# Row sums from ones beside the values, and the key masks prepared inside self attention, in a two-layer decoder kernel

## The chip, the cores and the metric

The kernel runs on one core of one Trainium2 chip, as a single launch. The metric is the device time of one execution in microseconds (us); the time given for a kernel is the median of its runs. The profile comes from one execution that the hardware profiler recorded. Its engines are PE (the matrix engine; PEld is its weight load), DVE (VectorE), ACT (ScalarE), POOL (GpSimd) and SP (SyncE, which here only issues transfers).

## The reference, cut to what matters

A decoder of two layers works on 4 batches of 256 tokens by 256 features, with 1601 memory tokens for each batch. Layer 0 is self attention, attention over the memory and a quantised feed-forward; layer 1 is a recurrence, cross attention and experts. The change lies in layer 0's first two parts:

```python
def _L0_attn_ref(x, ...):                 # 16 heads of 16
    q = (_layernorm(x, qn_g, qn_b) @ Wq + bq)...
    kv = (_layernorm(x, kvn_g, kvn_b) @ Wkv + bkv)...
    k, v = (kv[0], kv[1])
    q = _rotary(q * scale, x); k = _rotary(k * scale, x)
    qn = _layernorm(q, ln_g, ln_b)
    kn = _layernorm(k, ln_g, ln_b)
    scores = jnp.einsum('bhqd,bhkd->bhqk', qn, kn) / jnp.sqrt(hd)
    scores = jnp.where(causal, scores, jnp.finfo(scores.dtype).min)
    w = jax.nn.softmax(scores, axis=-1)
    a = jnp.einsum('bhqk,bhkd->bhqd', w, v)
    return a.transpose(0, 2, 1, 3).reshape(B, C, Dm) @ Wo + bo

def _L0_xattn_ref(hidden_states, memory_tokens, memory_mask):
    scores = jnp.einsum('bsd,bmd->bsm', hidden_states, memory_tokens) * scale
    scores = jnp.where(memory_mask[:, None, :], scores, neg_inf)
    attn = jax.nn.softmax(scores, axis=-1)
    readout = jnp.einsum('bsm,bmd->bsd', attn, memory_tokens)
    valid_b = jnp.any(memory_mask, axis=-1)
    return jnp.where(valid_b[:, None, None], readout, jnp.zeros_like(readout))
```

## The kernel before, in words

Everything of a batch stays on the chip: `xs[b]` holds its 256 tokens as two blocks of 128 partitions. For each batch a Python generator `before(b)` (L934) emits self attention (L336), memory attention (L524), feed-forward (L633) and recurrence (L694), one stage between two `yield`s. A loop of ticks takes one stage of each running generator per tick; the batches start at ticks 0, 3, 9 and 15 (`START`). Three further streams are woven in: `shared_weights` (L303) from tick `TERN` = 20 on, the position tables and the first head's keys of layer 1's cross attention (`angles`, L959, and `before_head`, L1128) from tick `SIDE` = 24 on, and then the cross attention's heads and the experts, which are about four fifths of the time.

The order of the work on each engine is not the order in which it is written. The tile framework's scheduler puts instructions into the engines' queues from the order of emission, the data and the free buffers; each queue then runs strictly in that order. `behind` (L1344) ties everything that one stage of a stream emits behind the instruction that each engine was given last, so that the scheduler can't pull it forward. `shared_weights` and the position streams go through it.

Self attention of a batch, in stages:

- Statistics, normalisation, and transposes to features (L342 to L359).
- The query and key product `pq` and its bias add `qk` (L367, L371), the value product `pv` and its add `v` (L377, L381). Rotary and the norm of every head follow on VectorE and POOL (L391 to L415).
- Transposes to `tp_q` and `tp_k`; `qm` (L426, L427) and `kT` (L430) are made from them. For batch 0 the small table `qln` is made here.
- Four groups of four heads (c, e in 0, 1). A group makes the scores of 4 heads x 256 queries x up to 256 keys in two PSUM tiles of two banks each (L445 adds the causal mask by a matmul, L451 the scores). VectorE takes the negative maxima `mx` (L455, L456). ScalarE takes the exponentials (L463), each with an accumulated row sum, which the profile shows as a second instruction, ACTIVATION_READ_ACCUMULATOR; `V.reciprocal` inverts the eight sums (L467). PE transposes the weights into `tpp` (L474) and `tpq` (L480); ScalarE copies `tpp` out (L475) and VectorE `tpq` (L483). PE multiplies by the values into `po` (L489, L492); of the 32 columns of values that one matmul takes, 16 are the head's and 16 its neighbour's, whose result is not used. ScalarE copies `po` (L496), PE transposes it back into `tb` (L500) and VectorE multiplies by the inverted sums into `a` (L502).
- The output projection `pw` (L516) and the residual add (L520).

Memory attention (L524) first prepares the key mask: the mask's bytes come by two transfers on SP's queue into `mk` (L530, L531), VectorE makes `mf` and `cnt` from them (L533, L535), PE turns both into `xpm` (L537), and VectorE copies them out as `mb`, the bias of each key, and `ok`, which tells whether a batch has any key (L542). `mb` is read by the score copies (L565), `ok` only at the very end of a batch's memory attention, by `s1` (L618), which scales the readout `xpo` (L607) on its way into x (L620). `mb` and `ok` have two buffers each, `mk`, `mf` and `cnt` one.

`shared_weights` makes the feed-forward's two weights ternary: for each, a sum of absolute values (L309), a product with ones (`pgg`, L311), and twice a comparison and a combination (L323, L324); then the table `kron` of the recurrence.

PSUM has eight banks. Until the last batch has finished self attention, four are a ring for tiles of one bank (`p1`: `pq`, `pv`, `tpp`, `tpq`, `po`, `tb`, `pw`, `xpm`, `pgg` and others) and four make two tiles of two banks (`p2`: scores). After that (`second_part`, L149) the latter are given to other tiles of one bank.

## Time and profile before

| what | value |
|---|---|
| median of 3 runs | 1831.21 us (1830.79 to 1831.85) |
| the profiled execution | 1831.5 us, of it a span of 1829.5 us |
| PE busy | 1727.7 us, 94% |
| VectorE busy | 1300.5 us, 71% |
| ScalarE busy | 1008.2 us, 55% |
| POOL busy | 872.4 us, 48% |
| mean granted PE clock | 0.968 |
| first 320 us: PE busy | 258.4 us |

The profile's page gives the busy time of each engine, then the span in 40 slices of 45.7 us with the busy share in tenths, and the chain of work that ended last. A group line names the line of the kernel, the engine, the operation, what is written from what, and its shape; then the count, the time in all and the mean of one in ns, and the idle time of the engine before it with what ended that. In rows in order of time, the first two numbers are start and length in us. A row of windows gives for each stretch the busy time of each engine, with the number of instructions, then the clock that the throttle granted to PE (1.00 is full), the share of the DMA engines and their rate.

### The profile page before, as it was taken

What the parts mean: (1) busy time and instruction counts of PE and PEld (TensorE: products, weight loads), DVE (VectorE), ACT (ScalarE), POOL (GpSimd) and SP (SyncE); (2) the same over time, 40 slices, a digit from 0 to 9 for tenths busy, and PEclk for the clock granted to TensorE, in tenths of its full rate; (3) what the DMA queues carried; (4) which work ended last, traced back from release to release, by engine and by line L of the source; (5) the groups of instructions that cost most, each with busy time, mean ns of one, the idle gap of its engine ahead of it and who ended that gap; (6) DMA issues with size and microseconds to landing.
All of it is one profiled execution on the core that took longest, in us unless ns stands there. A gap on an engine that the chain in (4) does not pass through costs nothing.

```text
span 1829.5 us, 20298 instructions
## 1 busy us (share of the span) xinstructions
PE 1727.7 (94%) x6576; PEld 1054.0 (58%) x6576; DVE 1300.5 (71%) x2444; ACT 1008.2 (55%) x1896; POOL 872.4 (48%) x716
## 2 busy tenths in 40 slices
PE   3779899989999999999999999999999999999997
PEld 2456686655555555555555555656565655556555
DVE  6785647786777678777767786767768676766764
ACT  1556636463666565665656565565656465555541
POOL 2100232111266566656657475555656565655470
PEclk8689999989999999999999999999999999999998
DMA  4001241100210101102020211111120211011001
GB/s 140 1 22 34 71 120 62 32 24 12 81 55 9 58 26 41 38 29 66 13 67 27 64 32 52 53 38 43 41 67 29 72 32 58 21 41 49 30 29 35
DMA packets 66217, 83.01 MB, mean 45 GB/s; under 512 B 6460, under 2 KB 49600, under 8 KB 66112
## 3 DMA queue, kind: packets, MB, share of 16 engines
q1 hardware_dynamic: 64960, 80.31, 14.4%
q10 hardware_dynamic: 1152, 1.41, 0.2%
q8 instruction: 53, 0.87, 0.2%
q14 instruction: 52, 0.43, 0.1%
HBM read 80.65 MB, written 1.05 MB: 45 GB/s over the span
## 4 chain that ended last, share of the span: by engine, by line
PE 70%; DVE 10%; ACT 8%; POOL 7%; issue 4%; DMA 0%; POOLq 0%; ACTq 0%; DVEq 0%
PE bsc L1181 17%; PE bpo L1221 17%; PE pk L1115 11%; POOL sum L1212 4%; PE mph L914 2%; PE bpw L1241 2%; ACT s L1206 2%; PE xsc L562 2%; ACT s L1182 2%; PE xpo L607 2%; PE pq L1078 1%; PE mpe L925 1%; ACT sm L463 1%; POOL ropeq L1040 1%; ACT ropeq L1047 1%
## 5 line engine op out<-in xcount | busy, mean ns | idle before, releaser
L1212 POOL TENSOR_TENSOR sum<-sum,s 128x512 f32<-128x512 f32 (+1 forms) x416 | 541.0, 1300 | 82.1 <-ACT s L1206 55.8
L1181 PE MATMUL bsc<-qTb,kTb 128*128 128x512 f32 (+1 forms) x960 | 457.9, 597 | 2.7 <-ACT kTb L1126 2.7
L1221 PE MATMUL bpo<-s,vb 128*128 128x512 f32 (+1 forms) x960 | 459.1, 596 | 0.0
L1182 ACT ACTIVATE s<-bsc,kn 128x512 f32<-128x512 f32 (+1 forms) x480 | 317.7, 684 | 219.9 <-PE bsc L1181 209.4
L1186 DVE SCALAR_TENSOR_TENSOR acc<-bsc,kn,acc 128x512 f32<-128x512 f32 x448 | 333.9, 745 | 120.9 <-ACT s L1182 107.6
L1203 DVE TENSOR_TENSOR s<-s,bc 128x1024 f32<-128x1024 f32 (+1 forms) x256 | 289.4, 1143 | 16.8 <-PE bc L1199 16.7
L1206 ACT ACTIVATE s<-s 128x1024 f32<-128x1024 f32 (+1 forms) x256 | 255.8, 1005 | 47.8 <-DVE s L1203 46.1
L1181 PEld LDWEIGHTS bsc<-qTb,kTb 128*128 128x128 f32 (+1 forms) x960 | 173.5, 187 | 185.7 <-issue 141.7
L1221 PEld LDWEIGHTS bpo<-s,vb 128*128 128x128 f32 (+1 forms) x960 | 173.5, 191 | 132.7 <-issue 127.5
L1040 POOL TENSOR_TENSOR ropek<-ropek,ropuk 128x512 f32<-128x512 f32 (+1 forms) x64 | 78.2, 1222 | 242.3 <-DVE ropuk L1035 242.3
L1115 PE MATMUL pk<-wkv,cTk 128*128 128x256 f32 x832 | 190.1, 379 | 0.0
L1115 PEld LDWEIGHTS pk<-wkv,cTk 128*128 128x128 f32 x832 | 156.8, 190 | 28.3 <-issue 6.9
L1209 POOL TENSOR_TENSOR sum<-s 128x512 f32<-128x512 f32 x32 | 41.6, 1301 | 196.8 <-ACT s L1206 196.8
L1047 ACT ACTIVATE ropeq<-ropeq,rnq 128x128 f32<-128x128 f32 x128 | 41.5, 390 | 115.0 <-POOL rnq L1043 115.0
L1034 DVE TENSOR_TENSOR ropek<-pk,ctabk 128x256 f32<-128x256 f32 (+1 forms) x128 | 51.6, 403 | 55.6 <-ACT squares L1033 55.1
L1033 ACT ACTIVATE squares<-pk 128x256 f32<-128x256 f32 (+1 forms) x128 | 47.5, 373 | 64.7 <-PE pk L1115 41.6
L1118 ACT COPY vb<-pk 128x256 f32<-128x256 f32 (+1 forms) x128 | 46.0, 359 | 51.3 <-DVE ropuk L1035 48.5
L1184 DVE TENSOR_SCALAR acc<-bsc,kn 128x512 f32<-128x512 f32 x32 | 24.0, 749 | 62.8 <-ACT s L1182 62.8
L1241 PEld LDWEIGHTS bpw<-wo,aT 128*128 128x128 f32 x256 | 48.7, 191 | 34.2 <-issue 27.0
L463 ACT ACTIVATE sm<-sc,mx 128x128 f32<-128x128 f32 (+1 forms) x128 | 52.2, 436 | 27.3 <-DVE mx L456 20.2
L1241 PE MATMUL bpw<-wo,aT 128*128 128x256 f32 x256 | 66.3, 382 | 0.0
L1043 POOL TENSOR_TENSOR kn<-ssk,nhalf 128x4 f32<-128x4 f32 (+1 forms) x64 | 66.0, 1032 | 0.0
(487 smaller groups left out, 2483.8 us busy)
## 6 DMA issues: line engine op xcount, KB each, us to landing
cTk<-in_ctxT SPq DMA_DIRECT2D x32, 512.0 KB, 3.7
wq<-in_wq SPq DMA_DIRECT2D x16, 512.0 KB, 5.2
wo<-in_wo SPq DMA_DIRECT2D x16, 512.0 KB, 3.9
wi<-in_wi SPq DMA_DIRECT2D x32, 256.0 KB, 2.9
xcT<-in_ctxT SPq DMA_DIRECT2D x12, 512.0 KB, 3.7
xct<-in_ctx SPq DMA_DIRECT2D x12, 512.0 KB, 3.7
cTk<-in_ctxT SPq DMA_DIRECT2D x16, 384.0 KB, 3.2
wkv<-in_wkv SPq DMA_DIRECT2D x16, 256.0 KB, 3.8
```

The source lines that it names most:

```text
L463: A.activation(ex[:, h, k], scs[u][:, h, k], AF.Exp, bias=mx[:, j, i : i + 1], accum_out=sums[:, j, i : i + 1])
L1040: G.tensor_tensor(r4, r4, u4[:, :, ::-1, :], ALU.add)
L1043: G.tensor_tensor(rn, ss[:, 0:n], nhalf[:, 0:n], ALU.pow)
L1115: T.matmul(pk[:, q, :], lhsT=src, rhs=e["wkv"][:, c, :], start=c == 0, stop=c == 1)
L1181: T.matmul(pc[0:n, :], lhsT=e["kT"][:, k * P : k * P + n], rhs=q, start=True, stop=True)
L1182: A.activation(s[0:n, i, :], pc[0:n, :], AF.Copy, scale=e["kn"][0:n, k : k + 1])
L1186: V.scalar_tensor_tensor(self.acc[0:n, :], pc[0:n, :], e["kn"][0:n, k : k + 1], self.acc[0:n, :], ALU.mult, ALU.max)
L1203: V.tensor_tensor(s[0:n, 0:w, :], s[0:n, 0:w, :], self.bc[0:n, None, :].to_broadcast([n, w, 512]), ALU.subtract)
L1206: A.activation(s[0:n, 0:w, :], s[0:n, 0:w, :], AF.Exp)
L1212: G.tensor_tensor(self.sum[0:n, :], self.sum[0:n, :], s[0:n, i, :], ALU.add)
L1221: T.matmul(self.po, lhsT=e["v"][0:n, k, :], rhs=self.s[c][0:n, i, :], start=k == 0, stop=k == NCH - 1)
L1241: T.matmul(pw[:, j * 256 : j * 256 + 256], lhsT=aT[:, o : o + P], rhs=e["wo"][:, self.h + h, :], start=True, stop=True)
```

## The change

The values are no longer one tile of 512 columns per batch. Each block of 128 keys gets a place of 512 columns, 16 heads by 32: 16 values, then 16 ones. There are eight such places, two for each of the four batches; the ones are written once, at the start, by POOL, and the places lie in buffers that layer 1 uses later (three in `v`, three in `kT`, two `sum` tiles). The product `po` then holds, beside the 16 sums of weighted values of a head, the sum of its weights in 16 rows. So the exponentials need no accumulated sum; the reciprocal is taken from `tb` after the transposes back, from PSUM. The copies of `tpq` go from VectorE to ScalarE. The add of the values is two adds, one for each block.

`key_mask(b)` is a function of its own, called in self attention once `kT` is made, one stage before the first scores. `mf` and `cnt` are tied behind what VectorE was given last at that point, and so is `qln` of batch 0. `shared_weights` starts at tick 28 in place of 20. `behind` is written with the two helpers `latest` and `keep_behind`, and does what it did.

```diff
--- before.py
+++ after.py
@@ -32,7 +32,7 @@
 NA = 3
 NDB = 3
 NROPE = 3
-TERN = 20
+TERN = 28
 SIDE = 24
 SIDEN = 4
 RATE = 1
@@ -168,6 +168,18 @@
+    spots = [
+        w[:, 512 * i : 512 * (i + 1)]
+        for w in (
+            wk.tile([P, NCH * HD1], F32, tag="v", name="values0"), wk.tile([P, NKEY], F32, tag="kT", name="values1")
+        )
+        for i in range(3)
+    ] + [fr.tile([P, 512], F32, tag="sum", name=f"values{i}", bufs=2) for i in (2, 3)]
+    spots = [w.rearrange("p (h d) -> p h d", d=2 * HD0) for w in spots]
+    for w in spots:
+        G.memset(w[:, :, HD0:], 1.0)
     xs = [const.tile([P, 2, D], F32, tag=f"x{b}", name=f"x{b}") for b in range(B)]
     def load_x(b):
@@ -226,6 +238,21 @@
             V.bn_stats(st, xb[:, j, :])
             V.bn_aggr(mv[:, j, :], st)
         return mv
+    def latest():
+        ins = nc.cur_bb.bb.instructions
+        return {i.engine: i for i in ins}, len(ins)
+    def keep_behind(before):
+        last, n = before
+        for i in nc.cur_bb.bb.instructions[n:]:
+            if i.engine in ENGINES and i.engine in last:
+                tc.add_manual_dep(
+                    i, last[i.engine].name,
+                    mybir.DependencyInfo(mybir.DependencyClass.NoSync, mybir.DependencyReason.DATA), reason="order",
+                )
     def rsqrt(v, eps, nm, n=2):
@@ -370,7 +397,7 @@
                     )
             V.tensor_add(qk[:, j, :], pq, bqkv[:, 0:512])
             yield
-        v = fa(b, f"v{b}").rearrange("p (j d) -> p j d", j=2)
+        v = spots[2 * b : 2 * b + 2]
         pv = p1(f"pv{b}")
         for j in range(2):
             for c in range(2):
@@ -378,7 +405,11 @@
                     pv[:, j * 256 : j * 256 + 256], lhsT=xx[:, 1, c, j * P : (j + 1) * P], rhs=wqkv[:, c, 512:768],
                     start=c == 0, stop=c == 1,
                 )
-        V.tensor_add(v, pv.rearrange("p (j d) -> p j d", j=2), bqkv[:, None, 512:768].to_broadcast([P, 2, D]))
+        for j in range(2):
+            V.tensor_add(
+                v[j][:, :, 0:HD0], pv[:, j * 256 : j * 256 + 256].rearrange("p (h d) -> p h d", d=HD0),
+                bqkv[:, 512:768].rearrange("p (h d) -> p h d", d=HD0),
+            )
         hd = [P, 2, 32, HD0]
         q4 = qk.rearrange("p j (h d) -> p j h d", d=HD0)
@@ -417,10 +448,12 @@
         yield
         if b == 0:
+            so_far = latest()
             for e in range(2):
                 V.tensor_scalar(
                     qln[:, e, :], cols[:, 20:22], 1.0 / math.sqrt(HD0), cc("par")[:, e : e + 1], ALU.mult, ALU.mult
                 )
+            keep_behind(so_far)
         tq = to_features(qkn[:, :, 0:256], f"q{b}")
         qm = fb(b, f"qm{b}").rearrange("p (e n) -> p e n", e=2)
         V.tensor_scalar(qm[:, 0, :], tq, qln[:, 0, 0:1], qln[:, 0, 1:2], ALU.mult, ALU.add)
@@ -429,6 +462,7 @@
         kT = fa(b, f"kT{b}")
         A.activation(kT, tk, AF.Identity, bias=lnb, scale=lng)
         kT = kT.rearrange("p (c t) -> p c t", c=2)
+        key_mask(b)
         a = fa(b, f"a{b}").rearrange("p (j d) -> p j d", j=2)
         yield
         for c in range(2):
@@ -437,7 +471,6 @@
                 nm = f"{b}{c}{e}"
                 mx = sm([P, 2, 4], "mx4", f"mx{nm}", 4)
-                sums = sm([P, 2, 4], "sums", f"sum{nm}", 4)
                 scs, es = [], []
                 for u in range(2):
                     sc = p2(f"sc{nm}{u}")[0].rearrange("p (h k) -> p h k", h=2)
@@ -460,11 +493,8 @@
                     for h in range(2):
                         for j, k in enumerate((slice(0, 128), slice(128, 384))):
                             i = 2 * u + h
-                            A.activation(
-                                ex[:, h, k], scs[u][:, h, k], AF.Exp, bias=mx[:, j, i : i + 1], accum_out=sums[:, j, i : i + 1]
-                            )
+                            A.activation(ex[:, h, k], scs[u][:, h, k], AF.Exp, bias=mx[:, j, i : i + 1])
                     es.append(ex)
-                V.reciprocal(sums.rearrange("p j h -> p (j h)"), sums.rearrange("p j h -> p (j h)"))
                 yield
                 pT = fb(b, f"pT{nm}").rearrange("p (h t) -> p h t", h=4)
                 for u in range(2):
@@ -480,17 +510,17 @@
                         T.transpose(tp[:, (2 * u + h) * P : (2 * u + h + 1) * P], es[u][:, h, 256:384], ident)
                 for u in range(2):
                     src = tp[:, 2 * u * P : 2 * (u + 1) * P].rearrange("p (h t) -> p h t", h=2)
-                    V.tensor_copy(es[u][:, :, 384:512], src)
+                    A.copy(es[u][:, :, 384:512], src)
                 yield
                 po = p1(f"po{nm}")
                 for i in range(4):
-                    f = slice(c * P + 32 * i, c * P + 32 * i + 32)
-                    T.matmul(po[32 * i : 32 * i + 32, 0:256], lhsT=v[:, 0, f], rhs=pT[:, i, :], start=True, stop=False)
+                    h = 8 * c + 2 * i + e
+                    T.matmul(po[32 * i : 32 * i + 32, 0:256], lhsT=v[0][:, h, :], rhs=pT[:, i, :], start=True, stop=False)
                 for i in range(4):
-                    f = slice(c * P + 32 * i, c * P + 32 * i + 32)
+                    h = 8 * c + 2 * i + e
                     T.matmul(
-                        po[32 * i : 32 * i + 32, 128:256], lhsT=v[:, 1, f], rhs=es[i // 2][:, i % 2, 384:512], start=False, stop=True
+                        po[32 * i : 32 * i + 32, 128:256], lhsT=v[1][:, h, :], rhs=es[i // 2][:, i % 2, 384:512], start=False, stop=True
                     )
                 oT = es[0][:, 0, 0:256]
                 A.copy(oT, po[:, 0:256])
@@ -498,11 +528,13 @@
                 tb = p1(f"tb{nm}")
                 for j in range(2):
                     T.transpose(tb[:, j * P : (j + 1) * P], oT[:, j * P : (j + 1) * P], ident)
+                tb4 = tb[:, 0:256].rearrange("p (j r d) -> p j r d", j=2, r=4)
+                rs = sm([P, 2, 4], "sums", f"sum{nm}", 4)
+                V.reciprocal(rs, tb4[:, :, :, HD0])
                 for j in range(2):
                     V.tensor_mul(
                         a[:, j, c * P : (c + 1) * P].rearrange("p (r e d) -> p r e d", e=2, d=16)[:, :, e, :],
-                        tb[:, j * P : (j + 1) * P].rearrange("p (r e d) -> p r e d", e=2, d=16)[:, :, e, :],
-                        sums[:, j, :, None].to_broadcast([P, 4, 16]),
+                        tb4[:, j, :, 0:HD0], rs[:, j, :, None].to_broadcast([P, 4, 16]),
                     )
                 yield
         G.tensor_tensor(xb, xb, bo[:, None, :].to_broadcast([P, 2, D]), ALU.add)
@@ -521,18 +553,22 @@
         yield
-    def memory_attention(b):
-        xb = xs[b]
-        last = S2 - 12 * P
+    last = S2 - 12 * P
+    masks = {}
+    def key_mask(b):
+        so_far = latest()
         mk = sm([NC2, P], "mk", f"mk{b}", 1, U8)
         V.memset(mk, 0.0)
         nc.sync.dma_start(out=mk[0:12, :], in_=t["mask"][b, 0 : 12 * P].rearrange("(c p) -> c p", p=P))
         nc.sync.dma_start(out=mk[12:13, 0:last], in_=t["mask"][b : b + 1, 12 * P : S2])
+        so_far = so_far[0], latest()[1]
         mf = sm([NC2, P], "mf", f"mf{b}", 1)
         V.tensor_scalar(mf, mk, -1.0, -NEG, ALU.add, ALU.mult)
         cnt = sm([NC2, 1], "cnt", f"cnt{b}", 1)
         V.tensor_reduce(cnt, mk, AX.X, ALU.max)
+        keep_behind(so_far)
         pm = p1(f"xpm{b}")
         T.transpose(pm[:, 0:NC2], mf, ident[0:NC2, 0:NC2])
         T.matmul(pm[:, 64:65], lhsT=cc("ones")[0:NC2, :], rhs=cnt, start=True, stop=True)
@@ -540,6 +576,11 @@
         V.tensor_copy(mb, pm[:, 0:NC2])
         ok = sm([P, 1], "ok", f"ok{b}")
         V.tensor_scalar(ok, pm[:, 64:65], 1.0, None, ALU.min)
+        masks[b] = mb, ok
+    def memory_attention(b):
+        xb = xs[b]
+        mb, ok = masks[b]
         mv = moments(xb, f"xa{b}")
         r1 = rsqrt(mv[:, :, 1], 1e-5, f"xa{b}")
         yield
@@ -1343,18 +1384,9 @@
     def behind(gen, end=None):
-        ins = nc.cur_bb.bb.instructions
-        n = len(ins)
+        before = latest()
         said = next(gen, end)
-        latest = {}
-        for i in ins[:n]:
-            latest[i.engine] = i
-        for i in ins[n:]:
-            if i.engine in ENGINES and i.engine in latest:
-                tc.add_manual_dep(
-                    i, latest[i.engine].name,
-                    mybir.DependencyInfo(mybir.DependencyClass.NoSync, mybir.DependencyReason.DATA), reason="order",
-                )
+        keep_behind(before)
         return said
```

## The prediction

> **What bounds the kernel now.** The page comes first: engine totals, the slices, the chain.

> ```profile
> PE 1727.7 (94%) x6576; PEld 1054.0 (58%) x6576; DVE 1300.5 (71%) x2444; ACT 1008.2 (55%) x1896; POOL 872.4 (48%) x716
> PE   3779899989999999999999999999999999999997
> PEclk8689999989999999999999999999999999999998
> PE 70%; DVE 10%; ACT 8%; POOL 7%; issue 4%; DMA 0%; POOLq 0%; ACTq 0%; DVEq 0%
> ```

> PE is full from the eighth slice (about 320 us) on. I compared the queues of the two built programs: from the last matmul of batch 3's memory readout (322 us in this trace) every engine has the same instructions in the same order to the end. So only the first 322 us can change, and what they gain or lose moves the rest as a block. Next, the windows of that part (each row: PE, PEld, DVE, ACT, POOL busy, then the granted clock):

> ```profile
> 20.00:40.00 20.00, 8.48 (x28) 6.37 (x28) 17.71 (x37) 3.17 (x5) 7.31 (x6) 0.70 0.02 3
> 100.00:120.00 20.00, 15.45 (x143) 10.13 (x147) 19.40 (x50) 12.81 (x49) 1.48 (x2) 0.92 0.14 41
> 120.00:140.00 20.00, 15.88 (x111) 10.84 (x108) 16.30 (x33) 11.31 (x44) 0.00 (x0) 0.74 0.17 53
> 140.00:160.00 20.00, 18.71 (x181) 12.20 (x180) 14.01 (x41) 14.63 (x58) 0.71 (x1) 1.00 0.10 29
> 160.00:180.00 20.00, 18.04 (x120) 12.47 (x119) 8.76 (x36) 11.65 (x43) 0.70 (x1) 0.91 0.01 1
> 280.00:300.00 20.00, 20.00 (x73) 12.93 (x72) 14.62 (x29) 13.78 (x18) 2.90 (x2) 1.00 0.18 59
> ```

> VectorE leads at 20 to 40 us (17.71 of 20) and at 100 to 120 (19.40); from 140 on it has room. PE idles most where VectorE is full. The instructions in time order show how (VectorE at 19 and 110 to 115 us, PE at 117 and 124):

> ```profile
> 10.76 1.00 DVE L357 TENSOR_SCALAR xqkv<-tp_sa,cols 128x256 f32<-128x256 f32 x2 [1.84 <-PE tp_sa L271]
> 19.04 0.21 DVE L533 TENSOR_SCALAR mf<-mk 13x128 f32<-13x128 uint8 x1 [7.28 <-DMA mk<-in_mask]
> 19.56 0.69 DVE L371 TENSOR_TENSOR qk<-pq,rows 128x512 f32<-128x512 f32 x1
> ...
> 111.49 1.27 DVE L324 SCALAR_TENSOR_TENSOR wfc<-wfc,hig,negg 128x1024 f32<-128x1024 f32 x1
> 114.70 0.68 DVE L456 TENSOR_REDUCE mx<-sc 128x2 f32<-128x512 f32 x1
> ...
> 117.24 0.80 PE L445 MATMUL sc<-trib,identb 128*128 128x384 bf16 x2 [4.14 <-ACT sm L463]
> 124.53 0.58 PE L311 MATMUL pgg<-partg,cst 128*128 128x1 f32 x2 [3.30 <-DVE partg L309]
> ```

> VectorE sits 7.28 us on a mask transfer with queries behind it; later a ternarising step stands ahead of a maximum that the exponentials, and through them PE, wait for. Last, the costs of what the change touches, and PE's waits between 60 and 330 us (us in total, times, longest):

> ```profile
> L463 ACT ACTIVATE sm<-sc,mx 128x128 f32<-128x128 f32 (+1 forms) x128 | 52.2, 436 | 27.3 <-DVE mx L456 20.2
> 139.81 0.20 ACT L463 ACTIVATION_READ_ACCUMULATOR sm<-sc,mx 128x1 f32 x1
> 139.90 0.37 ACT L463 ACTIVATE sm<-sc,mx 128x128 f32<-128x128 f32 x1
> L483 DVE COPY sm<-tpq 128x256 f32<-128x256 f32 x30 | 11.5, 416 | 8.3 <-PE tpq L480 8.2
> PE sc L445 <- ACT sm L463: 10.6, 10, 4.1
> PE tpp L474 <- ACT sm L463: 6.6, 4, 3.8
> ```

> **The change, part by part.** The sum starts from the profiled execution's 1831.5 us (span 1829.5 and 2.0 around it), 0.3 us above the median of the runs.

> 1. *Mask wait.* Before, batch 0's L533 stands fourth from the front on VectorE; after, it stands behind the query product (L426, 49.3 us here), long after its transfer. The first qk add (L371) ran at 19.56; its eight matmuls stood at the head of a block of 16 from 11.36 to 16.5 us, so it can start near 14. Gain 5.5 at most. From it comes off the 0.6 us of L533, L535 and the copies that now stand in VectorE's busy 40 to 55 us, and at worst 2 us of PE waiting there for the mask product. I take -4.5, between -5.5 and -3. Late next is the POOL root at 22.89, which needs VectorE's own statistics and moves with them. On SP the masks now stand ahead of the positions and, for batches 2 and 3, of the weights win; SP's issues are 0.3 to 0.8 us each and what they pass is used after 90 us: nothing, 0.5 at worst.

> 2. *Reads and copies on ScalarE.* 128 accumulator reads go. The listing gives 0.2 us each, but the next instruction starts 0.09 us after a read starts (139.81, 139.90): 128 x 0.09 = 11.5 us really leave ScalarE. The 32 tpq copies come: at the 0.34 us from start to start that they take on VectorE, 10.9; bounds 8 and 13.3 (32 x 0.416). ScalarE is left even (-3.5 to +2). VectorE loses 10.9.

> 3. *Reciprocal.* 16 x 0.2 us on VectorE before and after, but it now follows the transpose tb and stands ahead of the two products: 0.2 to 0.3 us later per group, mostly under the next group's work: +1, between 0 and +4. The split value adds (two of about 0.42 us for one of 0.68) add 0.6 us over four batches; the eight fills of ones, by the 0.2 us row of a half as wide fill, are under 3.3 us in POOL's idle 3.5 us before its first cast: nothing.

> 4. *Ternarising eight ticks later, and VectorE's relief.* It is 2 x 2.28 + 4 x 1.27 + 4 x 0.74 = 12.6 us of VectorE, from about 103 to 142 us to about 150 to 180, where 17 us of 40 are idle. At 98 to 125 us PE's gaps of 1.25, 4.14 and 3.30 us stand against VectorE, and a half clock follows (0.50 from 116.68 to 130.34), worth 13.66/2 = 6.8 us at PE's full work. Most: 8.7 + 6.8 = -15.5, with a little of the later gaps -17. Least: the queue of exponentials takes over as the limit; ScalarE has 12.8 and 11.3 of 20 there, so that at least a third of the gaps goes: -3. I take -9, nearer the middle since the matmuls behind the gaps also wait on each other in turn.

> 5. *PSUM.* The mask products now come early, but the small tiles mb and ok have two buffers. ok2 must wait till batch 0's readout has used ok0 (L618, about 270 us), ok3 for ok1. Until then xpm2 and xpm3 each hold one of the four banks of the shared ring, from about 92 and 127 us. In the built program every later ring tile up to the readout alternates between two banks, and after xpo0 has one. From this trace I paired each tile's first write with its last read: between 137 and 229 us 1.85 banks are held on average, more than two 27% of the time, 33 bank-us beyond two. If each excess stood in line alone: about +17. Walking seven groups through two banks by their fills and holds (copies of tpp held 1.3 us, tpq 1.4, po 1.0, tb 1.4) gives 5.2 us a group where 139.2 to 175.0 now takes 35.8/7 = 5.1: +0.7 there, +2 to +3 for the later stretch. Bounds 0 and +17; I take +4, near the walk.

> 6. *Clock.* Half rate at 174.71 to 178.12 follows a gap of 1.47 us only. Two more such stretches, 2 x 3.41/2, would be 3.4; bounds 0 and +5; I take +1.

> 7. *Angles.* Batch 0's position tables (about seven VectorE operations of 960 elements, 1.15 us each by L1004) are ordered behind ok3 and so move from 130 to 265 us to after 270. VectorE is idle 16 of the 40 us from 260 to 300, and PE is at 20.00 of 20: +1, between -2 and +3. If that cover is gone, batch 1's x (L620) is late for PE. One more table load on ScalarE, 1.28 us: +0.3 (0 to 1.3).

> Sum: -4.5 + 0 + 1 - 9 + 4 + 1 + 1 + 0.3 = -6.2, so 1825.3, or 1825.0 against the median.

> [...]

> **The rivals.**

> - *PSUM decides (slower).* Two banks make PE wait for evacuation on ScalarE, which now does three of the four kinds. For it: 53% of 137 to 150 us holds three or more banks. Against: 165 to 210 holds under 1.65 on average. It decides once steps 5 and 6 exceed 11.2 us together. With +13, +5 and step 4 at -7: -4.5 + 1 - 7 + 13 + 5 + 1.3 = +8.8, 1840.
> - *Only the mask wait pays (no change).* Each group's chain (max, exponential, transpose, copy, product) keeps the rate: step 4 at -3, the costs at +6.5: -1.0, 1830.
> - *The full relief.* Gaps and half clock vanish, the banks suffice: -5.5 - 14 + 2 = -17.5, 1814.
> - *The change does not do what it says:* for batches 2 and 3 the mask is not ready with the keys, ok2 and ok3 come as late as before. That is step 5's price, not a time of its own.

> **How the numbers follow.** Forecast 0.45 (1820 to 1827); PSUM 0.28; only the mask 0.15; full relief 0.12. 0.2% is 3.7 us, about what a measurement here can tell from none. Faster 0.45 + 0.12 = 0.57, same 0.15, slower 0.28. The range goes to 1843, leaving the worst third of the PSUM case out, and down to 1811, the full relief with a little over: some 0.15 outside.

> **What would show it.** Step 1: no idle time of VectorE on the mask, the first exponential 4 to 5 us earlier. Step 4: no gap over 2 us between 98 and 125, clock near 1.0 there. Step 5: new waits of PE's tpp, tpq, po or tb on ScalarE copies or on VectorE between 130 and 270 us. Wrong if the windows from 130 to 230 us take over 10 us longer for the same matmuls.

## The result, and the profile after

The changed kernel takes 1844.24 us, median of 7 runs (1836.07 to 1848.52), against 1831.17 us before (7 runs, 1830.25 to 1831.85): a ratio of 1.0061, with a 95% interval of 1.0041 to 1.0082. (The ratio is taken over all the runs, not from the two medians; three single runs far out, at 1893, 2604 and 4608 us, are left out of the ratios below.) It is slower; 1825.0 with a range to 1843 was forecast. Its runs also spread over 12 us, where those of the kernel before lay within 2; over the sessions of the experiments the kernel before itself ran from 1825.2 to 1832.9 us. The profiled execution took 1844.24 us, its span 1842.5.

The page of the changed kernel (engine totals, the two slice lines that answer to those shown of before, the chain):

```profile
PE 1741.5 (95%) x6576; PEld 1059.7 (58%) x6576; DVE 1291.3 (70%) x2416; ACT 1007.9 (55%) x1801; POOL 871.7 (47%) x724
PE   4789898998999999999999999999999999999996
PEclk8786999999999999999999999999999999999998
PE 72%; DVE 10%; ACT 8%; POOL 7%; issue 3%; DMA 1%; ACTq 0%; POOLq 0%; DVEq 0%; SPq 0%
```

PE has the same 6576 matmuls and is busy 13.8 us longer. VectorE lost 9.2 us, ScalarE nothing (1008.2 before, 1007.9 now). The windows (PE, PEld, DVE, ACT, POOL busy, granted clock):

```profile
20.00:40.00 20.00, 9.19 (x28) 6.96 (x28) 18.08 (x38) 3.75 (x6) 6.28 (x5) 0.74 0.02 4
100.00:120.00 20.00, 15.76 (x134) 10.12 (x132) 14.63 (x43) 12.49 (x33) 0.00 (x0) 0.87 0.12 40
120.00:140.00 20.00, 17.75 (x119) 11.24 (x117) 6.32 (x15) 13.76 (x38) 0.00 (x0) 0.84 0.01 1
140.00:160.00 20.00, 19.36 (x106) 10.15 (x104) 9.38 (x23) 8.25 (x23) 0.00 (x0) 0.50 0.00 0
160.00:180.00 20.00, 20.00 (x114) 12.18 (x115) 11.61 (x26) 9.13 (x24) 0.88 (x1) 0.68 0.09 27
280.00:300.00 20.00, 20.00 (x82) 14.40 (x81) 16.25 (x42) 14.42 (x22) 4.57 (x5) 1.00 0.34 104
```

From 140 to 160 us PE is busy 19.36 of 20 us and gets through 106 matmuls; before it did 181 in 18.71. The clock is 0.50 where it was 1.00: the trace has half clock without a break from 138.7 to 172.8 us, 34 us. The instructions in order of time (VectorE early on, then PE from 133 to 144 us), and then the waits of PE between 60 and 330 us:

```profile
10.48 0.99 DVE L384 TENSOR_SCALAR xqkv<-tp_sa,cols 128x256 f32<-128x256 f32 x2 [2.97 <-PE tp_sa L298]
14.90 0.69 DVE L398 TENSOR_TENSOR qk<-pq,rows 128x512 f32<-128x512 f32 x1 [3.42 <-PE pq L394]
47.22 0.17 DVE L576 COPY mb<-xpm 128x13 f32<-128x13 f32 x1 [0.50 <-PE xpm L574]
...
133.71 1.09 PE L504 MATMUL tpp<-cst,sm 128*128 128x128 f32 x8
136.13 0.48 PE L478 MATMUL sc<-trib,identb 128*128 128x384 bf16 x2 [1.32 <-ACT sm L496]
141.88 1.97 PE L504 MATMUL tpp<-cst,sm 128*128 128x128 f32 x8
```

```profile
PE sc L478 <- ACT sm L496: 8.4, 6, 3.1
PE xpo L648 <- DVE x L661: 6.6, 1, 6.6
PE tpp L504 <- ACT sm L496: 5.6, 2, 4.2
```

The second row is PE's wait, near 320 us, for a batch's x at the end of the readouts. Of the kernel before:

```profile
PE xpo L607 <- DVE x L620: 3.6, 1, 3.6
```

The mask wait is gone: qk's add starts at 14.90 in place of 19.56. PE's gaps between 98 and 125 us shrank from 8.7 to 4.2 us. But at 141.88 eight transposes take 1.97 us that took 1.09 at 133.71. PE's idle time from 60 to 300 us, added up from the trace, is 24.7 us, before 25.5, and up to the last readout matmul (346.7 us, before 332.8) 31.3, before 29.5: PE hardly waits more, it works slower. Half clock between 60 and 340 us adds up to 71.7 us, before to 44.4; half of the difference is 13.7 us, an estimate of its price, and the span is 13.0 us longer. Half clock did not always cost its half, though: behind the last readout matmul the changed kernel has 12.5 us less of it (27.8 against 40.3) and is only 1.0 us quicker (1495.8 against 1496.8). What ScalarE does now, between 60 and 320 us:

```profile
L496 ACT ACTIVATE sm<-sc,mx 128x128 f32<-128x128 f32 x120 | 40.8, 440 | 29.0 <-DVE mx L489 26.3 <-DVE nr_hf L270 2.7
L513 ACT COPY sm<-tpq 128x256 f32<-128x256 f32 x30 | 9.8, 387 | 4.0 <-PE tpq L510 4.0
L488 DVE TENSOR_REDUCE mx<-sc 128x2 f32<-128x256 f32 x30 | 12.6, 418 | 30.6 <-PE sc L484 30.6
```

The third row is VectorE's: it now sits idle 30.6 us before the maxima, waiting for PE's scores; before it was 7.7. The relief of VectorE happened, and PE became what it waits for.

Against the kernel before, by the end of the maxima of the 16 groups (worked out from VectorE's L456 and L489 rows): 2.3 us ahead at the first, 1.1 at the second, 5.8 at the eighth (121.9 us), 4.8 at the tenth, then 1.2 behind at the eleventh, 7.9 at the thirteenth and 11.9 at the sixteenth. All of the loss arises between 136 and 228 us: from the eighth maxima to the sixteenth it takes 106.0 us, before 88.2.

### The profile page after: what moved, and what is told of

Its sections match the earlier page's. It is cut to its first block, busy times and chain, and to the rows that moved or that the text cites. A ratio compares the mean times of both kernels' runs of the same rounds, so it can differ in the third digit from the quotient of the medians.

```text
span 1842.5 us, 20188 instructions
## 1 busy us (share of the span) xinstructions
PE 1741.5 (95%) x6576; PEld 1059.7 (58%) x6576; DVE 1291.3 (70%) x2416; ACT 1007.9 (55%) x1801; POOL 871.7 (47%) x724
## 4 chain that ended last, share of the span: by engine, by line
PE 72%; DVE 10%; ACT 8%; POOL 7%; issue 3%; DMA 1%; ACTq 0%; POOLq 0%; DVEq 0%; SPq 0%
PE bsc L1222 17%; PE bpo L1262 17%; PE pk L1156 11%; POOL sum L1253 4%; PE mph L955 2%; PE bpw L1282 2%; ACT s L1247 2%; PE xpo L648 2%; PE xsc L603 2%; ACT s L1223 2%; PE pq L1119 1%; PE mpe L966 1%; PE sc L484 1%; POOL ropeq L1081 1%; ACT ropeq L1088 1%
## 5 line engine op out<-in xcount | busy, mean ns | idle before, releaser
L1247 ACT ACTIVATE s<-s 128x1024 f32<-128x1024 f32 (+1 forms) x256 | 255.8, 1006 | 47.0 <-DVE s L1244 45.4
L1282 PEld LDWEIGHTS bpw<-wo,aT 128*128 128x128 f32 x256 | 49.2, 193 | 34.4 <-issue 27.8
L1286 DVE SCALAR_TENSOR_TENSOR x<-bpw,rs,x 128x256 f32<-128x256 f32 x128 | 55.5, 474 | 13.2 <-PE bpw L1282 13.0
```

The costliest lines, as they stand in the source:

```text
L1247: A.activation(s[0:n, 0:w, :], s[0:n, 0:w, :], AF.Exp)
L1282: T.matmul(pw[:, j * 256 : j * 256 + 256], lhsT=aT[:, o : o + P], rhs=e["wo"][:, self.h + h, :], start=True, stop=True)
```

## The experiments

The theories, guesses for the runs to test. *P*: the two held PSUM banks thin out PE's work and with it the clock. Rivals: *S*, the tpq copies on ScalarE do it; *C*, it is chance how the clock's windows fall; later *A*, what stands behind ok2 and ok3 on VectorE; *W*, plain waiting for banks; and on the granted clock itself *G*, it goes by the array's work, against *T*, it goes by busy time. "us" below is the ratio's distance from 1 times 1831, so that kernels from different chips can be set against each other; each ratio is against runs of the kernel before on the same chip. Where a ratio's interval is needed it stands in the table:

| run | median us | ratio to before | us |
|---|---|---|---|
| the changed kernel | 1844.24 | 1.0061 [1.0041, 1.0082] | +11.2 |
| e1 four buffers | 1830.16 | 1.0002 [0.9994, 1.0011] | +0.4 |
| e2 tpq on VectorE | 1834.15 | 1.0023 [1.0012, 1.0035] | +4.2 |
| e3 masks early, four buffers, tick 20 | 1839.11 | 1.0049 [1.0037, 1.0061] | +9.0 |
| e4 masks early, two buffers, tick 28 | 1836.06 | 1.0031 [1.0019, 1.0042] | +5.7 |
| e5 dense fill | 1841.80 | 1.0067 [1.0048, 1.0085] | +12.3 |
| e6 thin fill | 1845.97 | 1.0084 [1.0069, 1.0100] | +15.4 |
| e7 tick 28 alone | 1832.29 | 1.0010 [1.0001, 1.0019] | +1.8 |
| e8 four buffers, tick 20 | 1823.85 | 0.9966 [0.9953, 0.9978] | -6.2 |
| e9 rows alone | 1824.56 | 0.9969 [0.9956, 0.9982] | -5.7 |
| e10 as e8, tpq on VectorE | 1832.42 | 1.0013 [1.0001, 1.0025] | +2.4 |
| e11 as e3, dense fill | 1839.76 | 1.0057 [1.0044, 1.0071] | +10.4 |
| e12 as e3, thin fill | 1840.97 | 1.0061 [1.0048, 1.0074] | +11.2 |
| e13 as e1, two banks held | 1839.57 | 1.0051 [1.0039, 1.0063] | +9.3 |
| e14 as e1, one bank held | 1836.21 | 1.0024 [1.0013, 1.0035] | +4.4 |
| e15 as e8, tick 24 | 1829.72 | 0.9996 [0.9987, 1.0004] | -0.7 |
| e16 as e8, tick 16 | 1834.20 | 1.0025 [1.0015, 1.0035] | +4.6 |

### The banks: e1, then e13 and e14

e1 is the changed kernel with

```diff
-        mb = sm([P, NC2], "mb", f"mb{b}")
+        mb = sm([P, NC2], "mb", f"mb{b}", 4)
-        ok = sm([P, 1], "ok", f"ok{b}")
+        ok = sm([P, 1], "ok", f"ok{b}", 4)
```

> The changed kernel with four buffers in place of two for each of mb and ok, so that xpm2 and xpm3 are let go at once and the ring keeps its four banks. Theory P (two banks make matmuls and score tiles alternate so that PE never shows the clock gate a dense stretch): the half-clock stretch of 34 us at 139 to 173 us is gone (none longer than 14 us after 130 us), 1821 to 1829 us, and the spread of the runs falls below 3 us. Theory S (the tpq copies on ScalarE do it): still 1838 to 1848 with a stretch of over 20 us. Theory C (the stretch is a matter of how the gate's windows of 3.41 us fall on the work, whatever the banks): runs spread over 8 us or more again.

1830.16 us, all within 1.7 us of each other. Four small buffers more take back 10.8 of the 11.2 us, and the 34 us stretch is gone. The windows from 140 to 180 us of the changed kernel, then of e1:

```profile
140.00:180.00 40.00, 39.36 (x219) 22.33 (x217) 20.99 (x48) 17.39 (x46) 0.88 (x1) 0.59 0.05 14
```

```profile
140.00:180.00 40.00, 34.93 (x276) 24.50 (x267) 27.99 (x68) 22.72 (x63) 0.71 (x1) 0.87 0.14 41
```

PE is busy 39.36 us for 219 matmuls at 0.59 there, 34.93 for 276 at 0.87 here. S falls for this step, the copies being on ScalarE in both, and so does C as it was put for this run: it asked for a spread of 8 us or more, and e1's runs lie within 1.7. P's time was put at 1821 to 1829; that e1 is no faster than the kernel before has another cause, below. Since the buffers also free what waits for ok2 and ok3, e13 takes e1 and holds the banks alone:

```diff
+        if b in (2, 3):
+            held[b] = p1(f"hold{b}")
+            T.matmul(held[b][:, 0:1], lhsT=cc("ones")[0:NC2, :], rhs=cnt, start=True, stop=True)
...
         V.tensor_scalar(s1, s1, ok, None, ALU.mult)
+        if b + 2 in held:
+            V.tensor_scalar(sm([P, 1], "seen", f"seen{b}"), held[b + 2][:, 0:1], s1[:, 0:1], None, ALU.mult)
```

e14 does it for b = 3 only.

> The changed kernel with four buffers for mb and ok (1830.2 us), but with a tile of its own beside each of xpm2 and xpm3 that keeps a bank from there until batch 0's (batch 1's) s1 has been made, as ok2 and ok3 did; mb, ok, and the position tables stay free. Theory P (the held banks cost the 14 us): 1838 to 1850, runs spread over 5 us or more. Rival A (what stands behind ok2 and ok3 on VectorE costs it): 1829 to 1833.

> The same with one bank held, from xpm3 to batch 1's s1: three banks for the ring. Theory P: between the two, 1831 to 1838. Rival A: 1829 to 1833.

No bank held +0.4, one +4.4, two +9.3 us: both times lie where P put them. But the traces do not bear this out as a dose and its answer. In e14's profiled run (1836.16 us) the sixteenth maxima end at 215.8 us and the last readout matmul at 333.1, in e1 at 216.0 and 333.3, and half clock between 60 and 340 us is 54.6 us in both: while the one bank is held, nothing is lost. e14's span is 5.4 us longer, and nearly all of that comes in the last 40 us of the run, where its queues have the experts' last matmuls in another order. From 1800 us to the end, first e1, then e14:

```profile
1800.00:1829.00 29.00, 21.14 (x92) 17.11 (x90) 14.34 (x41) 3.07 (x8) 0.00 (x0) 0.97 0.12 37
```

```profile
1800.00:1835.00 35.00, 24.33 (x94) 19.01 (x92) 15.15 (x46) 3.27 (x9) 0.00 (x0) 0.84 0.10 31
```

Of e14's eleven runs that count, three lie at 1830.7 to 1830.9 us, two at 1832.8 and six from 1836.2 to 1839.1. In e13 the loss does fall while the banks are held: its last readout matmul ends at 342.8 us, 9.5 later than e1's. Yet it does not fall where the changed kernel loses. From the eighth maxima to the sixteenth e13 takes 95.3 us, as e1 does, and the changed kernel 106.0; e13 loses 3.2 us ahead of that stretch and 6.3 behind it. Its half clock between 60 and 340 us is 68.3 us, but no stretch of it behind 130 us is longer than 13.7. PE's windows of e13:

```profile
140.00:180.00 40.00, 37.59 (x257) 22.69 (x250) 26.91 (x64) 22.29 (x59) 0.71 (x1) 0.83 0.12 33
```

So e1 shows that the two buffers cost this kernel its 11 us, and e13 that two held banks alone can cost about as much. That the held banks make the stretch of 34 us is not shown. From e13 to the changed kernel another 1.9 us stay, inside the two intervals, but that does not bound A, since the two kernels lose at different places. One loss goes with the two buffers and not with held banks: PE's wait for x is 6.6 us in all five profiled kernels with the early masks and two buffers (the changed one, e2, e4, e5, e6), and 3.5 or 3.6 in the thirteen others, e13 among them. Ahead of that x, in these five alone, the product of s1 with ok lasts 2.3 us in place of 0.23, beside an instruction of POOL that lasts 2.35 (316.9 us in the changed kernel). Why the two buffers bring them together is not shown. The runs of e13 lie within 2.5 us, so the spread that was expected with P did not come; what makes it is open (e8, with no bank held, spreads over 8.8).

### The row part alone, and the masks: e9, e8, e3, e4

e9 is the kernel before with the values beside ones, the sums from po and the tpq copies on ScalarE, and nothing of the masks or the tick. e8 is e1 with `TERN = 20`, so e9 plus the early masks without held banks. e3 is the kernel before plus the early masks with four buffers; e4 the same with two buffers and tick 28.

> The kernel before with the values beside ones, the row sums from po and the tpq copies on ScalarE, nothing else: masks prepared in memory attention, ternarising at tick 20. If the time of the kernel with four buffers and tick 20 (1823.9 us) is the mask wait plus VectorE's relief, the relief alone is worth 3 to 5 us: 1826 to 1828. If the row part gives nearly all of it and the mask wait is absorbed by 66 us, as the traces suggest: 1822 to 1825. If both only pay together: 1829 to 1834.

> The changed kernel with four buffers for mb and ok and ternarising at tick 20 as before. If later ternarising gave most of the gain up to 125 us that the changed kernel shows (5.8 us ahead at the eighth group's maxima), this one is level with before there, and 1831 to 1838 at the end. If VectorE's relief from the tpq copies and the reciprocal gave it, it is ahead by 3 us or more there, 1826 to 1831.

The row part alone makes the kernel faster by 5.7 us, about as much as e8 (6.2). e9 lies where its second range put it; e8 is faster than both of its ranges, and at the eighth maxima it is 5.6 us ahead, as its second one asks. e8 beats both kernels of this case: 0.9966 [0.9953, 0.9978]. Its windows where the changed kernel lost:

```profile
100.00:140.00 40.00, 33.69 (x303) 23.07 (x301) 33.03 (x80) 27.56 (x77) 0.00 (x0) 0.87 0.20 61
140.00:180.00 40.00, 36.35 (x282) 24.72 (x280) 18.53 (x55) 26.30 (x73) 1.40 (x2) 0.96 0.01 3
```

The clock is 0.96 from 140 to 180 us, and VectorE carries its 33 us before that, at 100 to 140, not after.

> The kernel before with only the masks moved into self attention (with their order and that of qln), four buffers for mb and ok, ternarising at tick 20 as before: the mask part of the change without the held banks, the values and row sums as before. By all theories VectorE's 7.28 us wait is gone; 4 to 5 us of it reach the end if the half-clock stretches fall as before: 1826 to 1828. Theory C allows 1820 to 1840.

> The kernel before with the masks moved and two buffers for mb and ok as in the change, ternarising at tick 28; values, row sums and tpq copies as before. Theory P: the held banks alone make it slow, 1836 to 1850, with a half-clock stretch of over 20 us between 130 and 230. Theory S: 1822 to 1830, since the copies stay on VectorE and the accumulated sums stay.

e3 missed by 11 us, and only C has room for it: the masks alone, with no bank held, make the kernel 9 us slower. It is 2.4 us ahead at the first maxima and 8.2 behind at the tenth, with half clock from 117.9 to 145.2 us. With the row part (e8 against e9) the same step is worth 0.5 us, within the intervals. The 4.7 us that qk's add comes earlier are thus never seen at the end. e4, with two buffers and the later tick, is not slower than e3 with four (+5.7 and +9.0), so held banks need not decide in every order. Its time lies at the lower edge of P's range, and the stretch that P asked for is not in its trace; that trace is of its quickest run (1831.56 of 1831.56 to 1837.62 us), which is level with the kernel before at the last readout matmul (332.9 and 332.8).

### The tick of the ternarising: e7, e15, e16

One line each: `TERN = 28` in the kernel before (e7), `TERN = 24` and `TERN = 16` in e8.

> The kernel before with ternarising from tick 28 in place of 20 and nothing else. By step 4 of the prediction: PE's gaps of 4.14 and 3.30 us between 113 and 125 us go, and part of the half clock behind them: 1820 to 1828. Theory G: the gaps go too, but half-clock windows come where ternarising now falls (150 to 180 us) or not, as the work per window decides: 1824 to 1840.

> Four buffers, ternarising from tick 24. If its cost grows with the tick, as it moves from the stretch where PE waits on the maxima into the one where PE is full: 1825 to 1829. If tick 28's 6 us are an accident of one order: anywhere from 1821 to 1832.

> Four buffers, ternarising from tick 16. If the cost grows with the tick: 1819 to 1824, the best of all so far. If tick 20 is the best place: 1824 to 1830.

In the kernel before the later tick costs 1.8 us, where step 4 promised a gain. With four buffers: +4.6 us at tick 16, -6.2 at 20, -0.7 at 24, +0.4 at 28. It does not grow with the tick; tick 20 is the best of the four. e15 lies just above its first range and inside its second, e16 above both of its own. e7 is 4.9 us ahead at the eighth maxima, as foreseen, and 1.5 behind at the fourteenth: PE has new gaps of 2.03 us at 144 and 2.28 at 179, each with 6.8 us of half clock behind it. At tick 16 PE waits 5.0 us in one piece for partg, as the waits between 60 and 140 us say:

```profile
PE sc L478 <- ACT sm L496: 9.9, 5, 3.8
PE pgg L338 <- DVE partg L336: 5.0, 1, 5.0
```

### The tpq copies: e2, e10

```diff
-                    A.copy(es[u][:, :, 384:512], src)
+                    V.tensor_copy(es[u][:, :, 384:512], src)
```

> The changed kernel with the tpq copies back on VectorE. Theory P: the banks are still held, so 1836 to 1850 us and a half-clock stretch of over 20 us between 130 and 230. Theory S: the stretch goes, 1822 to 1830. ScalarE loses about 11 us of work and VectorE gains as much, which by either theory alone is worth under 4 us.

> Four buffers, tick 20, and the tpq copies back on VectorE (the row sums still from po). By step 2 ScalarE is left even by the exchange and VectorE gets 10.9 us back: 2 to 5 us slower than with the copies on ScalarE, 1826 to 1829. If ScalarE is the tighter engine now, faster: 1819 to 1823.

In e8's order the copies on ScalarE are worth 8.6 us (e10), more than expected; e10's runs stand in two groups, 1826.4 to 1827.7 and 1831.8 to 1834.7 us. In the changed kernel they cost 7.0 (e2). Its 1834.15 us lie between the ranges of P and S, and its longest half-clock stretch behind 130 us is 13.7, in a run of 1838.78: neither theory has it, and the engine of the copies also decides how the work falls together. An edit has no price of its own here, only one in an order.

### The granted clock and the array's work: e5, e6, e11, e12

In the traces of the two kernels every stretch of one clock but the last is a whole number of times 3.41 us long (before, half clock once from 174.71 to 178.12; after, ten times from 138.72 to 172.85), so I took the clock in windows of 3.41 us. For each window between 20 and 340 us of all 18 profiled kernels I added up the matmuls' work from their rows in the trace: the columns that each streams, in us at full clock (256 f32 columns start 0.216 us apart there, and 0.427 at half clock; 384 of bf16 take 0.17), times the part of the array that the row's shape gives (a score matmul has 32 of 128 rows, one of po 32 of 128 columns, but four of po's start within 0.02 us of each other and so count as the whole array together). The weighting by parts is my choice; no row shows it. Then, over 1687 windows, what clock the next one had:

```
array work in the window    next at half    next at full
below 1.08 us                    332             15
1.08 to 1.33 us                   76             44
1.33 us and more                   0           1220
```

The two bounds were set on these same windows and say nothing of others. They are the same whether the window itself ran at half or at full clock. With one bound at 1.23 us, 46 of the 1687 windows fall on the wrong side; with the best bound on busy time 164 do. Busy time tells less: of 180 half-clock windows in which PE was busy 99% or more, 51 were followed by half clock again. In the changed kernel the window at 135.3 us, still at full clock, has 1.32 us of work; the nine from 138.7 to 166.0 have 0.78 to 1.21, with PE busy all through eight of them; the one at 169.4, in which pw and po stand together, 1.56, and the next is full again. A half-clock window holds at most 1.71 us, half of 3.41, so the table's 1.08 to 1.33 us are 63% to 78% of it. That half clock would keep itself up where scores and small products alternate was my estimate from this; the changed kernel's windows agree with it, no run shows it by itself. A busy window alone was not enough here, as the 51 of 180 say.

All this is a correlation in these traces. The test adds matmuls into score tiles that the causal mask then overwrites, on the whole array or (thin) with 32 columns of weights, at the same places of every queue:

```diff
+                    if (b, c, e) in ((3, 0, 0), (3, 0, 1)):
+                        for i in range(4):
+                            T.matmul(sc[:, i % 2, 0:384], lhsT=ident, rhs=cst[:, 0:384], start=True, stop=True)
```

Thin: `sc[0:32, i % 2, 0:384]` and `lhsT=ident[:, 0:32]`. e11 and e12 do it in e3 with `range(2)` at (0, 1, 1) and (2, 0, 1).

> The changed kernel with 16 matmuls of 128x384 on the whole array added, 8 ahead of the scores of each of batch 3's first two groups (about 136 to 170 us), into score tiles that the causal mask then overwrites: more work for PE, the same result. Theory G (full clock is granted after a window of 3.41 us with enough array work, each matmul weighted with the part of the array that it fills; the scores fill little, so that half clock keeps itself up): the half-clock stretch of 34 us shrinks to 14 us or less and the time falls to 1832 to 1840 us in spite of 2.6 to 10 us of added work. Theory W (PE waits for the two banks, the clock only follows): the added work costs its time, 1846 to 1854, the stretch stays over 24 us.

> The control to the dense fill: the same 16 matmuls at the same places in every queue, but with 32 columns of weights, a quarter of the array, for the same streaming time. Theory G: they do not count enough, the stretch stays at 24 us or more and the time is 1843 to 1856, 6 us or more above the dense fill. Theory T (the gate counts busy time, not work) and theory W: within 3 us of the dense fill.

> The early masks with four buffers (e3: 1837.3 to 1840.0 us, half clock for 27 us from 118 us, no bank held) and 8 more matmuls of 128x384 on the whole array, 4 ahead of the scores of batch 0's last and batch 2's second group (about 118 to 140 us), overwritten by the causal mask. Theory G: the half-clock stretch there ends sooner (14 us or less in the profiled run) and the time falls to 1829 to 1836 in spite of the added work. Theory T (busy time counts) or W (waits count): no gain, 1838 to 1843.

> The control: the same 8 matmuls, at the same places in the queues, on a quarter of the array (32 columns). Theory G: 1837 to 1843, at least 3 us above the dense fill, and the half clock there stays over 17 us. Theory T: as the dense fill, within 2 us.

The dense fill took the 34 us stretch away (6.8 us at 140.8), but the thin one did too (6.8 at 145.2), and no time was won: +12.3 and +15.4 us, intervals overlapping, with 41.0 and 58.0 us of half clock between 60 and 340; +10.4 and +11.2 in e3's order, with 51.2 us in both. The fills themselves displace the scores. Each of the four runs missed a number of G: the two dense fills the time, the two thin ones (e6 and e12, whose times lie in G's ranges) the distance to the dense fill and the long stretch. W falls, since the stretch of over 24 us that it asked for in e5 did not stay. T has e12 (0.8 us from its dense fill, under 2 asked) and just misses e6 (3.1, under 3).

The traces of e6 and e12 tell why the control was none. By the part of the array, two windows with thin fills in e6 (131.5 and 134.9 us) hold 1.06 us of work each and two in e12 (121.0 and 138.1) 0.66 and 0.76, and all four were followed by full clock. Counted as if each fill took the whole array, they hold 2.07, 3.22, 1.62 and 1.47 us, and the three windows with thin fills that half clock followed (e12, 117.6, 131.3 and 134.7) hold 0.35, 1.17 and 1.04: then all seven fit the table. So in these seven windows the count that fits takes 32 columns of weights on all 128 rows in full, and weighting by columns is wrong for them; that the 32 rows of a score matmul count as a quarter stays a correlation. Nor are the 3 us between e5 and e6 the fills' doing: their queues differ in the fills' width alone, and e6 is already 3.2 us behind at the eighth maxima (124.1 and 120.9 us), ahead of the first fill. That much is chance between two runs.

How much of the loss the clock causes was not measured by itself. What speaks for it is the sum above (13.7 us of clock, idle time nearly unchanged) and the spread: the changed kernel's runs go from 1836.07 us at a mean clock of 0.968 to 1848.52 at 0.961, and 0.007 of 1846 us is 12.9. Over the 18 profiled kernels, time and half clock between 60 and 340 us go together only loosely (correlation 0.67).

## Why the prediction was wrong

Set one behind the other, four runs add up to the measured +11.2 us: the row part -5.7 (e9), the early masks -0.5 (e9 to e8), the later tick +6.6 (e8 to e1), two buffers in place of four +10.8 (e1 to the changed kernel). The prediction had -8 for the row part and the tick together (steps 2 to 4), where these give +0.9; -4.5 for the masks (step 1); and +6.3 for what the two buffers do (steps 5 to 7). So the step that failed most is step 4, by about 9 us; the buffers' steps were 4.5 short and step 1 4 too good. In another order of the parts the shares would be others: the tick alone costs 1.8 us in the kernel before.

The rival "PSUM decides", 0.28, at 1840 us, named the two buffers' effect as what decides and came near in its number, the latter by luck: it had +19.3 for steps 5 to 7, where 10.8 were measured, and -10.5 for steps 1 to 4, where the runs give +0.4.

- *Step 5, PSUM*, +4 taken from the walk: measured +8.9 (e1 to e13) and +10.8 with all that two buffers do (e1 to the changed kernel). The failure is in the walk, which counts waits: it moved seven groups through two banks with fills and holds from full clock, 5.2 us a group. From the tenth group's maxima to the fourteenth's the changed kernel took 45.4 us, the one before 33.7. The bound of +17, by the occupied banks, held.
- *Step 6, clock*, +1 with +5 at most: 13.7 us more, half of 27.3 us of half clock. Steps 5 and 6 were summed as if apart. My reading is that they are one thing in the changed kernel: fewer banks, less work together in a window, half clock, and then less work still. No run shows it, and e13, where the long stretch did not come, leaves it open. Idle time of PE, which the steps counted, hardly changed. Where step 6 reckoned with two more stretches of 3.41 us, the clock is at half for 39 of the 92 us from 137 to 229 us, before for 10.
- *Step 4, ternarising and relief*, -9, the largest miss: two things of opposite sign in one term. The row part and the copies gave -5.7 with everything else left (e9). The later tick gave +1.8 (e7) and +6.6 (e8 to e1). I read VectorE's idle 17 us from 140 to 180 as free room. It was not: what PE and ScalarE do there hangs on maxima, and the stretch where the wait was foreseen to go did gain 4.9 us (e7) and gave them back some 50 us later.
- *Step 1, mask wait*, -4.5: right at its place (4.7 us at qk, 2.3 at the first maxima), wrong at the end (-0.5, e9 to e8; +9.0 in e3). What was named late next, POOL's root, moved along; what was not named is batch 1's own chain, which at the second maxima leaves 1.1 us, and the mask work put into it (mf, cnt and a wait of 0.50 us ahead of 47.22, again 0.98 ahead of 59.68).
- *Step 2, ScalarE*, left even: its busy time is (1008.2, 1007.9). But "even" was not nothing: e10 prices the move of the copies alone at 8.6 us in e8's order.
- *Step 3* was not tried alone. *Step 7*, the tables behind ok3, +1, was not tried alone either. PE does not wait for batch 1's x (283.6 us), as was feared there, but 3.0 us longer for a later one (319.8 us).

Of its list of signs, that of step 1 came by half (the first maxima end 2.3 us earlier, where 4 to 5 were named), and the one for wrong came: "the windows from 130 to 230 us take over 10 us longer". The gaps between 98 and 125 us shrank to under 2 us, but the clock there was not near 1.0 (half from 114.8 to 125.1 us). The sign of step 5, new waits of PE's tpp, tpq, po or tb, did not come: between 60 and 330 us these four wait 7.2 us in all, before 8.0. The loss came almost without waits. Two readings were off without weight in the sum: the last readout matmul of the kernel before ends at 332.8 us (from 321.7 us on PE's queues are the same), and the ninth slice shows 8, not a full engine.

## What to carry to other kernels

A small tile that is prepared early but has too few buffers holds what it was made from: before moving a preparation, count how long every tile on its way, PSUM above all, now lives. Price a loss of overlap by the granted clock too, not only by idle time: here the half clock between 60 and 340 us grew from 44.4 to 71.7 us while PE's idle time from 60 to 300 us went from 25.5 to 24.7. When a loss grows with what was taken away, look up in the trace whether it falls where and while that is missing: e14's did not. And where an order is this sensitive, forecast the sign of a rearrangement with caution: moving the same copies to ScalarE won 8.6 us in one order and cost 7.0 in another.
